# VectorE's edge comparisons and scalings with one operand in PSUM, in a two-layer graph attention kernel

## The chip, the core and the metric

One Trainium2 chip; the program runs on one of its cores. The metric is the device time of one execution in microseconds (us). Times before come from three runs; the profile is of one further execution.

## What is computed

A graph of 6250 nodes and 100000 directed edges, sorted by target node, goes through a block: layer norm and ReLU of x (6250 x 768), two graph attention layers, two dense layers, and x is added at the end. Each attention layer adds an edge from every node to itself. Cut to what matters:

```python
def gat_conv(x, src, dst, W, a_src, a_dst, bias, heads):
    h = (x @ W).reshape(n, heads, -1)
    alpha_s = (h * a_src[None]).sum(-1)
    alpha_d = (h * a_dst[None]).sum(-1)
    e = jax.nn.leaky_relu(alpha_s[src] + alpha_d[dst], 0.2)
    m = jax.ops.segment_max(e, dst, num_segments=n)
    e = jnp.exp(e - m[dst])
    denom = jax.ops.segment_sum(e, dst, num_segments=n)
    alpha = e / (denom[dst] + 1e-16)
    out = jax.ops.segment_sum(h[src] * alpha[:, :, None], dst, num_segments=n)
    return out.reshape(n, -1) + bias
...
h = jnp.maximum(_layernorm(x), 0.0)
h = relu(gat_conv(h, src, dst, W1, a_src1, a_dst1, b1, 4))
h = relu(gat_conv(h, src, dst, W2, a_src2, a_dst2, b2, 1))
return x + relu(h @ Wm1 + bm1) @ Wm2 + bm2
```

## The kernel before

**First stage.** For each of 49 tiles of 128 nodes, x is loaded and normalized (ScalarE writes xn), turned by six TensorE transposes into a PSUM tile `tp` (four, then two; line 202), copied to SBUF by VectorE (`xT`, line 203), and multiplied by W1 together with the score vectors (`h_ps`, line 206). The 256 features of a node, a one for each head and the source scores go as one row of 264 numbers to a table in DRAM.

**Edges.** Each layer then goes over 784 tiles of 128 edges (782 hold edges), eight to a unit. For each tile GpSimd issues one indirect DMA (line 276) that gathers the 128 source rows by the indices in a column of `src_i`, an SBUF tensor, into G (five buffers of one unit each). The code of a turn i gathers unit i, matches unit i-1, weighs unit i-2 and spreads unit i-3; each engine works through its own queue in order, and a scheduler sets that order.

- `match`: VectorE compares a row of the edges' target places, broadcast over the partitions (`drow`, bf16), with the partition number (`pidx_b`, broadcast along the row) into `mask` (128 x 1024 bf16, line 294), and compares `iota` (0 to 127 along the row) with each edge's target place (`dcol`, one column per tile) into `hot` (128 x 1024 f32, line 298). TensorE multiplies `mask` by a window of target factors (`win`) into `e_ps` (PSUM): the target's factor for each edge.
- `weigh`: ScalarE takes two exponentials of the gathered source scores (`e1`, `e2`, lines 316 and 318). VectorE adds up the three bf16 parts of the factor (`rho`), multiplies (`v`), and takes the larger (`w`): the edge's unnormalized weight. In layer 1 `hw` is G times w (128 x 2080 f32, line 332); in layer 2 it is hot times w (128 x 1024 f32, line 328).
- `spread`: TensorE adds the weighted rows into the place of their target (`o_ps`, line 348, two PSUM tiles of four edge tiles each): hot by hw in layer 1, hw by G in layer 2. So G is last read by VectorE's `hw` in layer 1 and by TensorE's products in layer 2, and its buffer is then free for the gather five units later.
- `gather_up`: VectorE carries a running sum, `acc` = `acc` times a column `keep` + `o_ps` (line 363), and ScalarE copies 32 finished rows at a time into `sum` (line 374).

When 128 nodes are complete, further steps follow among the later units. In layer 1: add the node's own edge and divide (`mine`, `all_`, `o`, lines 427 to 434), transpose (`tp`, line 408), ReLU (`rT`), multiply by W2 (`h_ps`, line 441) and store a row of layer 2's table. In layer 2: the same for one head, with the bias added to the residual (`xt`, line 471), two dense layers (`m_ps`, line 484, `mT`, line 488; `y_ps`, line 498), the residual sum (`y`, line 500) and the store. Layer 2 gathers from a table that layer 1's last step completes, so the layers follow each other.

**PSUM** has eight banks of 2 KB per partition. One pool of two buffers per tag served the whole kernel: `tp` (transposes, `e_ps`), `mm` (`h_ps`, `m_ps`), `o` (`o_ps`), `y` (`y_ps`).

Of the kernel before, what the change touches and what calls it, by code (L numbers as in the profile page):

```python
# [9 lines left out]
F32 = mybir.dt.float32  # L10
BF16 = mybir.dt.bfloat16
# [5 lines left out]
P = 128  # L17
# [28 lines left out]
def kernel(  # L46
# [29 lines left out]
    ps = pool("ps", 2, space=bass.MemoryType.PSUM)  # L76

    def bcast(src, n, off=0):
# [72 lines left out]
    def with_scores(wp, W, WT, A, K, H, name):  # L151
# [7 lines left out]
        p = ps.tile([P, K, 2 * H], F32, name="aps", tag="tp")  # L159
# [19 lines left out]
    with tc.tile_pool(name="w1p", bufs=1) as wp, tc.tile_pool(name="x1", bufs=4) as xp, \  # L179
            tc.tile_pool(name="wk1", bufs=3) as wk:  # L180
        w1 = with_scores(wp, W1, W1T, A1, KI, 4, "w1")
        for i in range(NT):
# [21 lines left out]
            h_ps = ps.tile([P, HID + 8], F32, name="h_ps", tag="mm")  # L204
# [52 lines left out]
    def layer_edges(layer, H, steps, prefetch):  # L257

        C = HID // H
        with tc.tile_pool(name=f"pre{layer}", bufs=1) as pre, \  # L260
# [22 lines left out]
            def match(u):  # L283

                if u % 2 == 0:
# [8 lines left out]
                nc.vector.tensor_tensor(mask[:, t0 * P:(t0 + n) * P],  # L294
                                        drow[0][:, u % 2, t0 * P:(t0 + n) * P],
                                        pidx_b.to_broadcast([P, n * P]), ALU.is_equal)
                hot = eg.tile([P, 8, P], F32, name="hot", bufs=3)
                nc.vector.tensor_tensor(  # L298
                    hot[:, t0:t0 + n], iota.unsqueeze(1).to_broadcast([P, n, P]),
                    dcol[:, 8 * u + t0:8 * u + t0 + n].unsqueeze(2).to_broadcast([P, n, P]),  # L300
                    ALU.is_equal)
                e_ps = ps.tile([P, 8, 3 * H], F32, name="e_ps", tag="tp")
                for t in T:
                    g = 2 * u + t // TPG
                    nc.tensor.matmul(e_ps[:, t], mask[:, t * P:(t + 1) * P], win[:, g + 1],  # L305
                                     start=True, stop=True)
                return hot, e_ps

            def weigh(u, G, hot, e_ps):
# [13 lines left out]
                nc.vector.tensor_mul(v[:, T], e2[:, T], rho[:, T])  # L323
# [494 lines left out]
```

## Time and profile before

| | |
|---|---|
| median of the runs | 2580.2 us (2576.93 to 2584.65, 3 runs) |
| the profiled execution | 2569.64 us, span 2567.9 us |
| mean granted TensorE clock | 0.77 |
| TensorE busy (matmul) | 1429.3 us, 56% |
| VectorE busy | 1324.1 us, 52% |
| ScalarE busy | 448.5 us, 17% |
| GpSimd busy | 1761.1 us, 69% |
| DMA | 350.68 MB, mean 137 GB/s |

How to read the rows of the profile: a group's row has line, engine, operation, output and inputs with their sizes and the count, then busy time in us, the mean of one in ns, and after the second bar the idle time of its engine just before these instructions, with what ended it. A timeline's row has start, length (both us), engine, line, operation and, in brackets, the idle time before it and what ended that. PE is TensorE, DVE VectorE, ACT ScalarE, POOL GpSimd, SP the engine that issues most plain DMAs; "issue" is time in which the engine waited for nothing that the profile shows. Matrix products of f32 show two instructions each.

### The profile page before, as it was taken

The page shows a single profiled execution, that of the slowest core. Times are in us where ns is not written, and L with a number is a line of the kernel's source. Part 1 is how long each engine was busy: PE and PEld are TensorE (multiplying, and loading weights), DVE is VectorE, ACT ScalarE, POOL GpSimd, SP SyncE. Part 2 cuts the span into 40 slices and gives each one's busy share as a digit, 9 for nine tenths or more (in the row PEclk, how much of TensorE's full clock was granted, in tenths as well). Part 3 has the DMA queues.
Part 4 walks back from the last instruction along what each step waited for, and adds up shares of the span by engine and source line. Part 5 has one row for each costly group of instructions (what it writes and reads, how often), then busy time and mean ns, then how long its engine had stood idle before and what let it go on. Part 6 is the DMA issues. An engine that isn't in the chain of part 4 may idle for free. (4 is left out here: it accounts for less than half of the span.)

```text
span 2567.9 us, 22404 instructions
## 1 busy us (share of the span) xinstructions
PE 1429.3 (56%) x6784; PEld 1114.5 (43%) x6785; DVE 1324.1 (52%) x2458; ACT 448.5 (17%) x1434; POOL 1761.1 (69%) x1672
## 2 busy tenths in 40 slices
PE   5887335445445445445445464656666666666666
PEld 4665223334334334334334343445444544454444
DVE  5553445554554555555555633455555555555554
ACT  2442111111111111111111111111111111111111
POOL 0000777777777787778787377777777777777770
PEclk9999667677677677677677676877778777877788
DMA  4442444444444444444444445455555555555551
GB/s 164 127 127 74 117 118 127 117 127 129 118 125 130 118 123 131 123 119 127 116 124 121 138 116 154 137 162 168 167 167 167 168 166 167 168 168 166 167 159 57
DMA packets 142758, 350.68 MB, mean 137 GB/s; under 512 B 33570, under 2 KB 60194, under 8 KB 142628
## 3 DMA queue, kind: packets, MB, share of 16 engines
q0 software_dynamic: 75072, 209.10, 31.2%
q1 hardware_dynamic: 65540, 137.21, 16.2%
q10 hardware_dynamic: 2016, 2.85, 0.4%
q8 instruction: 56, 0.92, 0.1%
q14 instruction: 74, 0.61, 0.1%
HBM read 316.53 MB, written 32.50 MB: 136 GB/s over the span
## 5 line engine op out<-in xcount | busy, mean ns | idle before, releaser
L276 POOL DMA_INDIRECT G<-table,src_i x1564 | 1744.3, 1115 | 514.8 <-issue 455.8
L348 PE MATMUL o_ps<-G,hw 128*128 128x258 f32 x1564 | 438.0, 442 | 21.1 <-DVE hw L328 12.8
L363 DVE SCALAR_TENSOR_TENSOR acc<-acc,keep,o_ps 128x260 f32<-128x260 f32 (+1 forms) x390 | 185.6, 476 | 508.3 <-PE o_ps L348 508.0
L348 PE MATMUL o_ps<-hw,hot 128*128 128x260 f32 x1564 | 417.2, 426 | 54.5 <-DVE hw L332 52.3
L348 PEld LDWEIGHTS o_ps<-G,hw 128*128 128x128 f32 x1564 | 354.6, 230 | 109.1 <-issue 23.0
L348 PEld LDWEIGHTS o_ps<-hw,hot 128*128 128x128 f32 x1564 | 337.6, 219 | 123.8 <-DVE hw L332 57.7
L441 PE MATMUL h_ps<-w,rT 128*128 128x258 f32 x196 | 116.4, 699 | 446.8 <-ACT rT L411 446.8
L498 PE MATMUL y_ps<-wm,mT 128*128 128x384 f32 x392 | 180.7, 594 | 314.0 <-DMA G<-table,src_i 276.9
L441 PEld LDWEIGHTS h_ps<-w,rT 128*128 128x128 f32 x196 | 48.8, 307 | 460.2 <-ACT rT L411 459.9
L298 DVE TENSOR_TENSOR hot<-iota,dcol 128x1024 f32<-128x1024 f32 (+1 forms) x196 | 238.0, 1214 | 0.0
L294 DVE TENSOR_TENSOR mask<-drow,pidx_b 128x1024 bf16<-128x1024 bf16 (+1 forms) x196 | 237.3, 1212 | 0.1
L498 PEld LDWEIGHTS y_ps<-wm,mT 128*128 128x128 f32 x392 | 81.5, 222 | 352.8 <-ACT mT L488 319.0
L332 DVE TENSOR_TENSOR hw<-G,w 128x2080 f32<-128x2080 f32 (+1 forms) x98 | 226.8, 2314 | 0.7 <-DMA G<-table,src_i 0.3
L374 ACT ACTIVATE sum<-acc 32x260 f32<-32x260 f32 (+1 forms) x392 | 163.2, 416 | 228.4 <-DVE acc L363 220.9
L318 ACT ACTIVATE e<-G 128x32 f32<-128x32 f32 (+2 forms) x196 | 41.9, 214 | 788.9 <-DMA G<-table,src_i 781.2
L316 ACT ACTIVATE e<-G 128x32 f32<-128x32 f32 (+2 forms) x196 | 42.8, 218 | 778.1 <-DMA G<-table,src_i 682.1
L206 PE MATMUL h_ps<-w,xT 128*128 128x264 f32 x588 | 146.6, 400 | 37.3 <-DVE xT L203 37.3
L206 PEld LDWEIGHTS h_ps<-w,xT 128*128 128x128 f32 x588 | 110.5, 195 | 64.8 <-ACT sd L211 46.1
L408 PE MATMUL tp<-ident,o 128*128 128x128 f32 x196 | 41.9, 298 | 144.3 <-DVE v L323 103.0
L328 DVE TENSOR_TENSOR hw<-hot,w 128x1024 f32<-128x1024 f32 (+1 forms) x98 | 119.2, 1217 | 0.0
L305 PEld LDWEIGHTS <-mask 128*128 128x128 bf16 x1564 | 72.9, 102 | 80.1 <-issue 33.6
L408 PEld LDWEIGHTS tp<-ident,o 128*128 128x128 f32 x196 | 24.4, 147 | 178.8 <-issue 139.4
(384 smaller groups left out, 1002.3 us busy)
## 6 DMA issues: line engine op xcount, KB each, us to landing
drow<-dmod_d SPq DMA_DIRECT2D x98, 512.0 KB, 5.5
xt<-in_x SPq DMA_DIRECT2D x96, 384.0 KB, 3.6
G<-table,src_i POOLq DMA_INDIRECT x1564, 2.8
out<-y SPq DMA_DIRECT2D x48, 384.0 KB, 2.9
table<-row SPq DMA_DIRECT2D x49, 132.0 KB, 1.7
row<-table SPq DMA_DIRECT2D x49, 130.0 KB, 4.6
table<-row SPq DMA_DIRECT2D x49, 129.0 KB, 2.7
row<-table SPq DMA_DIRECT2D x49, 129.0 KB, 2.1
```

The source lines that it names most:

```text
L206: nc.tensor.matmul(h_ps, xT[:, k], w1[:, k], start=(k == 0), stop=(k == KI - 1))
L276: nc.gpsimd.indirect_dma_start(out=G[:, t], out_offset=None, in_=table[layer], in_offset=bass.IndirectOffsetOnAxis(ap=src_i[:, k:k + 1], a ...
L294: nc.vector.tensor_tensor(mask[:, t0 * P:(t0 + n) * P], drow[0][:, u % 2, t0 * P:(t0 + n) * P], pidx_b.to_broadcast([P, n * P]), ALU.is_equal)
L298: nc.vector.tensor_tensor(hot[:, t0:t0 + n], iota.unsqueeze(1).to_broadcast([P, n, P]), dcol[:, 8 * u + t0:8 * u + t0 + n].unsqueeze(2).to ...
L305: nc.tensor.matmul(e_ps[:, t], mask[:, t * P:(t + 1) * P], win[:, g + 1], start=True, stop=True)
L328: nc.vector.tensor_mul(hw[:, T], hot[:, T], w[:, T].to_broadcast([P, n, P]))
L332: nc.vector.tensor_mul(hw[:, T], G[:, T, :RW[1]].rearrange("p t (h c) -> p t h c", h=H), w[:, T].unsqueeze(3).to_broadcast([P, n, H, C + 1]))
L348: nc.tensor.matmul(o_ps, l, r, start=(t == T[0]), stop=(t == T[-1]))
L363: nc.vector.scalar_tensor_tensor(acc, run[0], keep[:, (g + 1) % 4:(g + 1) % 4 + 1], o[half], ALU.mult, ALU.add)
L374: nc.scalar.activation(done[t][r], acc[r], AF.Copy)
L441: nc.tensor.matmul(h_ps, rT[:, k], w2[:, k], start=(k == 0), stop=(k == KH - 1))
L498: nc.tensor.matmul(y_ps, mT[:, j], wm2[:, j, s * half:(s + 1) * half], start=(j == 0), stop=(j == KH - 1))
```

## The change

A copy of `iota` is kept in PSUM (`iota_ps`, f32, one bank). `mask` becomes a tensor-scalar operation on `drow` alone, with `pidx` (f32) as a column of scalars. `hot` is made in layer 1 only, from `iota_ps` and `dcol`. `rho`, `v` and, in layer 1, `w` live in PSUM, in three more parts of `e_ps`, so `hw` of layer 1 multiplies G (SBUF) by w (PSUM). In layer 2 `hot` and `hw` become one operation per edge tile, eight per unit: compare `iota_ps` with a column of `dcol`, times a column of `w`. PSUM is shared out anew: one bank for `iota_ps`, two for `e_ps` (tag `e`), two for `o_ps` and the first stage's `h_ps` (tag `o`), three for all else (tag `n`). The pool is closed before the rarely used general path (`general`), which gets one of its own. The diff, without the general path's:

```diff
-    ps = pool("ps", 2, space=bass.MemoryType.PSUM)
+    edges_stack = ExitStack()
+    ps = edges_stack.enter_context(tc.tile_pool(name="ps", bufs=2, space=bass.MemoryType.PSUM))
...
-    pidx_b = const.tile([P, 1], BF16, name="pidx_b")
-    nc.vector.tensor_copy(pidx_b, pidx)
...
+    iota_ps = ps.tile([P, P], F32, name="iota_ps", bufs=1)
+    nc.vector.tensor_copy(iota_ps, iota)
...
-                p = ps.tile([P, 4, P], F32, name="tp", tag="tp")
+                p = ps.tile([P, 4, P], F32, name="tp", tag="n", bufs=3)
...
-            h_ps = ps.tile([P, HID + 8], F32, name="h_ps", tag="mm")
+            h_ps = ps.tile([P, HID + 8], F32, name="h_ps", tag="o")
...
-                nc.vector.tensor_tensor(mask[:, t0 * P:(t0 + n) * P],
+                nc.vector.tensor_scalar(mask[:, t0 * P:(t0 + n) * P],
                                         drow[0][:, u % 2, t0 * P:(t0 + n) * P],
-                                        pidx_b.to_broadcast([P, n * P]), ALU.is_equal)
-                hot = eg.tile([P, 8, P], F32, name="hot", bufs=3)
-                nc.vector.tensor_tensor(
-                    hot[:, t0:t0 + n], iota.unsqueeze(1).to_broadcast([P, n, P]),
-                    dcol[:, 8 * u + t0:8 * u + t0 + n].unsqueeze(2).to_broadcast([P, n, P]),
-                    ALU.is_equal)
-                e_ps = ps.tile([P, 8, 3 * H], F32, name="e_ps", tag="tp")
+                                        pidx, None, ALU.is_equal)
+                hot = None
+                if layer == 1:
+                    hot = eg.tile([P, 8, P], F32, name="hot", bufs=3)
+                    nc.vector.tensor_tensor(
+                        hot[:, t0:t0 + n], iota_ps.unsqueeze(1).to_broadcast([P, n, P]),
+                        dcol[:, 8 * u + t0:8 * u + t0 + n].unsqueeze(2).to_broadcast([P, n, P]),
+                        ALU.is_equal)
+
+                e_ps = ps.tile([P, 8, 6 * H], F32, name="e_ps", tag="e")
...
-                rho = sm.tile([P, 8, H], F32, name="rho")
-                nc.vector.tensor_reduce(rho[:, T], e_ps[:, T].rearrange("p t (h k) -> p t h k", k=3),
-                                        AX.X, ALU.add)
-                v = sm.tile([P, 8, H], F32, name="v")
+                rho, v, w = (e_ps[:, :, k * H:(k + 1) * H] for k in range(3, 6))
+                nc.vector.tensor_reduce(
+                    rho[:, T], e_ps[:, T, :3 * H].rearrange("p t (h k) -> p t h k", k=3),
+                    AX.X, ALU.add)
                 nc.vector.tensor_mul(v[:, T], e2[:, T], rho[:, T])
-                w = sm.tile([P, 8, H], F32, name="w")
-                nc.vector.tensor_max(w[:, T], v[:, T], e1[:, T])
                 if layer == 2:
+                    w = sm.tile([P, 8, H], F32, name="w")
+                    nc.vector.tensor_max(w[:, T], v[:, T], e1[:, T])
                     hw = eg.tile([P, 8, P], F32, name="hw")
-                    nc.vector.tensor_mul(hw[:, T], hot[:, T],
-                                         w[:, T].to_broadcast([P, n, P]))
+                    for t in tiles(u):
+                        nc.vector.tensor_scalar(hw[:, t], iota_ps, dcol[:, 8 * u + t:8 * u + t + 1],
+                                                w[:, t], ALU.is_equal, ALU.mult)
                 else:
+                    nc.vector.tensor_max(w[:, T], v[:, T], e1[:, T])
                     hw = eg.tile([P, 8, H, C + 1], F32, name="hw")
...
-        p = ps.tile([P, KH, P], F32, name="tp", tag="tp")
+        p = ps.tile([P, KH, P], F32, name="tp", tag="n", bufs=3)
...
-            h_ps = ps.tile([P, HID + 2], F32, name="h_ps", tag="mm")
+            h_ps = ps.tile([P, HID + 2], F32, name="h_ps", tag="n", bufs=3)
...
-            m_ps = ps.tile([P, KH, P], F32, name="m_ps", tag="mm")
+            m_ps = ps.tile([P, KH, P], F32, name="m_ps", tag="n", bufs=3)
...
-                y_ps = ps.tile([P, half], F32, name="y_ps", tag="y")
+                y_ps = ps.tile([P, half], F32, name="y_ps", tag="n", bufs=3)
```

The scheduler orders the instructions anew; the orders that the prediction rests on stand in it.

More of the change, by code (lines that the diff above doesn't have):

```diff
@@ L158, in with_scores @@
         nc.sync.dma_start(a, A.rearrange("(j p) h -> p j h", p=P))
-        p = ps.tile([P, K, 2 * H], F32, name="aps", tag="tp")
+        p = ps.tile([P, K, 2 * H], F32, name="aps", tag="e")
         for k in range(K):
@@ L534, in general @@
     KH = HID // P
-    const, ps, dram, bcast, ident, sd, table = (
-        v[k] for k in ("const", "ps", "dram", "bcast", "ident", "sd", "table"))
+    const, dram, bcast, ident, sd, table = (
+        v[k] for k in ("const", "dram", "bcast", "ident", "sd", "table"))
     NTP = NT + 1
@@ L545, in general @@
         wk = pool("gwk", 1)
+        ps = pool("gps", 2, space=bass.MemoryType.PSUM)
         gdram = pool("gdram", 1, space=bass.MemoryType.DRAM)
@@ L769, in general @@
             for s in range(2):
-                y_ps = ps.tile([P, half], F32, name="y_ps", tag="y")
+                y_ps = ps.tile([P, half], F32, name="y_ps", tag="e")
                 for j in range(KH):
```

13 lines of the change are left out of this document (7 added, 6 removed).

## The prediction

> **What bounds the kernel now.** I read the page first: busy time in slices and the costliest groups. Then the view of one line, for the gather.
>
> ```profile
> POOL 0000777777777787778787377777777777777770
> ...
> L276 POOL DMA_INDIRECT G<-table,src_i x1564 | 1744.3, 1115 | 514.8 <-issue 455.8
> ```
>
> ```profile
> L276 POOL DMA_INDIRECT G<-table,src_i  x1564: 942/946/3459, 254.0 to 2508.2; - x196
> ...
>   issue: 455.8, 1496
>   DVE parts L230: 35.4, 1
> ```
>
> GpSimd issues 1564 gathers, one per tile of 128 edges, and has no other work from 254.0 us on. The idle time before them is 0.30 us each (455.8 over 1496), plus one gap of 35.4 us between the layers. So GpSimd never waits for buffers: from 254 to 2509.7 us the span is gathers laid end to end, and the slices of 7 and 8 are only that pause. The median gather takes 0.946 us but the mean 1.115: some are stretched. The windows by stage, for this line alone (length, busy time, count, clock, DMA share, GB/s), place that:
>
> ```profile
> 0.00:254.00 254.00, 0.00 (x0) 0.99 0.39 122
> 254.00:1418.60 1164.60, 926.65 (x782) 0.71 0.45 123
> 1418.60:1454.10 35.50, 0.07 (x1) 0.79 0.24 75
> 1454.10:2509.70 1055.60, 817.56 (x782) 0.78 0.56 162
> 2509.70:2567.90 58.20, 0.00 (x0) 0.83 0.14 49
> ```
>
> 782 gathers at 0.946 us would be 739.8 us. Layer 1 carries 926.65 - 739.8 = 186.9 us of stretch and layer 2 77.8: 264.7 us in all. The timeline of layer 1 tells whose it is:
>
> ```profile
> 1002.54 0.95 POOL L276 DMA_INDIRECT G<-table,src_i  x1 [0.31 <-issue]
> ...
> 1003.09 2.31 DVE L332 TENSOR_TENSOR hw<-G,w 128x2080 f32<-128x2080 f32 x1
> 1003.80 2.42 POOL L276 DMA_INDIRECT G<-table,src_i  x1 [0.30 <-issue]
> 1005.32 1.21 DVE L298 TENSOR_TENSOR hot<-iota,dcol 128x1024 f32<-128x1024 f32 x1
> ...
> 1006.52 0.95 POOL L276 DMA_INDIRECT G<-table,src_i  x1 [0.31 <-issue]
> ...
> 1007.08 1.21 DVE L294 TENSOR_TENSOR mask<-drow,pidx_b 128x1024 bf16<-128x1024 bf16 x1
> 1007.77 1.34 POOL L276 DMA_INDIRECT G<-table,src_i  x1 [0.30 <-issue]
> ```
>
> A gather that starts while VectorE runs `hw` ends at 1006.22, 0.82 us after `hw` does (1005.40); the one that starts in `mask` ends at 1009.11, again 0.82 after 1008.29. The gather that is under way when `hw` starts keeps its 0.95. So the gather needs something at its start that these instructions hold to their end, and the stretch is the end of the VectorE instruction less the gather's start less 0.13 us. Not every VectorE instruction does it. In layer 2:
>
> ```profile
> 2003.81 0.48 DVE L363 SCALAR_TENSOR_TENSOR acc<-acc,keep,o_ps 128x258 f32<-128x258 f32 x1
> 2003.88 0.95 POOL L276 DMA_INDIRECT G<-table,src_i  x1 [0.30 <-issue]
> ...
> 2019.77 1.09 DVE L500 TENSOR_TENSOR y<-y_ps,xt 128x384 f32<-128x384 f32 x2
> ...
> 2020.69 0.95 POOL L276 DMA_INDIRECT G<-table,src_i  x1 [0.30 <-issue]
> ```
>
> `acc` reads one tensor from SBUF, one from PSUM and a column of scalars from SBUF; `y` reads one of each memory. Gathers that start inside them are not stretched. `hw`, `hot` and `mask` read two tensors from SBUF.
>
> The Trainium skill, "SBUF — State Buffer", section "Who interferes with whom", has both halves of this: a VectorE instruction with two SBUF inputs contends with a GpSimd instruction that reads SBUF, and one with at most one does not. The same section infers that `tensor_tensor` does not stall a DMA issued from GpSimd; by that sentence the change would win nothing on the gathers, and the 2.42 us row decides against it.
>
> **The change, part by part.** Gathers, first term. After the change `hot` reads PSUM and SBUF, `hw` of layer 1 reads G from SBUF and its weights from PSUM, `hw` of layer 2 reads one PSUM tensor and two scalar columns, and `mask` reads one SBUF tensor. If only two SBUF tensors block, all of them leave the list: -264.7 us, for GpSimd is the path and nothing covers it.
>
> What stays, second term. Instructions with two SBUF tensors are still there, and their phases move. Rows for the sizes:
>
> ```profile
> L298 DVE TENSOR_TENSOR hot<-iota,dcol 128x1024 f32<-128x1024 f32 (+1 forms) x196 | 238.0, 1214 | 0.0
> L294 DVE TENSOR_TENSOR mask<-drow,pidx_b 128x1024 bf16<-128x1024 bf16 (+1 forms) x196 | 237.3, 1212 | 0.1
> L332 DVE TENSOR_TENSOR hw<-G,w 128x2080 f32<-128x2080 f32 (+1 forms) x98 | 226.8, 2314 | 0.7 <-DMA G<-table,src_i 0.3 <-DVE acc L363 0.3 <-DVE v L323 0.2
> ...
> L471 DVE TENSOR_TENSOR xt<-xt,bm2b 128x768 f32<-128x768 f32 x49 | 46.5, 948 | 5.4 <-DMA xt<-in_x 5.4
> ...
> L427 DVE TENSOR_TENSOR mine<-row,own 128x260 f32<-128x260 f32 x49 | 20.6, 419 | 0.0
> ...
> L194 DVE TENSOR_SCALAR shift<-mv,rstd 128x1 f32<-128x1 f32 x49 | 10.3, 211 | 1.5
> ...
> L123 DVE TENSOR_SCALAR far<-f 98x1024 f32<-98x1024 f32 x1 | 0.7, 686 | 0.0
> ```
>
> An instruction of L us at a random phase of the gathers' rhythm (0.946 + 0.30 = 1.25 us) costs (L - 0.13)²/2.5 on average; the most is L - 0.13. `xt` (0.948): 0.27 x 49 = 13 us, at most 40. `mine` (0.419) and its two neighbours of the same size: 0.033 x 147 = 5, at most 43. The one in layer 2 like `mine`: 2, at most 18. `mask` is now a one-tensor bf16 operation, which the trace lacks. From `hot` and `hw`: (2314 - 1214)/1056 = 1.04 ns an element and 0.15 us fixed. `far`, one f32 tensor, runs two elements in that time (0.686); a bf16 mask should be no slower, and if it halves once more it takes 0.41. So 0.41 to 0.69; I take 0.41. If it still blocks at a gather's start, 0.03 x 196 = 6, at most 55. Together 26, from 0 to 156. These phases are locked to the gathers, so each is all or nothing; I take 25.
>
> `hot` from PSUM and `hw` of layer 1: 258 elements in `acc` cost 0.48 us from PSUM against 0.419 for 260 in `mine`, so +0.06 each at most. Layer 2's `hot` (98 x 1.21) and `hw` (98 x 1.22) become 8 x 98 pieces of 128 elements: 0.13 us of elements at least, `shift`'s 0.211 plus 0.13 = 0.34 at most, so 1.1 to 2.7 us in place of 2.4 per unit. All of it lies beside the gathers; VectorE has room:
>
> ```profile
> 300.00:1400.00 1100.00, 507.94 (x2415) 393.47 (x2416) 567.80 (x944) 150.11 (x543) 875.18 (x739) 0.71 0.46 123
> ```
>
> (busy PE, weight loads, VectorE, ScalarE, GpSimd: VectorE 567.8 of 1100.) A unit (8 gathers) of layer 1 takes 1164.6/97.75 = 11.9 us and holds 6.2 us of VectorE work; the mask's 0.8 goes and 0.12 comes: 5.5, against 10 us of gathers. If that cover were gone, it would add up to 0.12 us a unit, 12 us per layer.
>
> The new PSUM pools, third term. Transposes get three buffers. TensorE in the first stage, two node tiles before the change (tp: transposes of the normalized x; h_ps: x times W1):
>
> ```order
> L202 MATMUL tp_519<-ident_63,xn_516 128x128 x4
> L202 MATMUL tp_525<-ident_63,xn_516 128x128 x2
> L206 MATMUL h_ps_529<-w1_132,xT_518 128x264 x6
> L202 MATMUL tp_558<-ident_63,xn_555 128x128 x4
> L202 MATMUL tp_564<-ident_63,xn_555 128x128 x2
> L206 MATMUL h_ps_568<-w1_132,xT_557 128x264 x6
> ```
>
> and the same two tiles after it:
>
> ```order
> L204 MATMUL tp_519<-ident_63,xn_516 128x128 x4
> L204 MATMUL tp_525<-ident_63,xn_516 128x128 x2
> L204 MATMUL tp_558<-ident_63,xn_555 128x128 x4
> L208 MATMUL h_ps_529<-w1_132,xT_518 128x264 x6
> L204 MATMUL tp_564<-ident_63,xn_555 128x128 x2
> L208 MATMUL h_ps_568<-w1_132,xT_557 128x264 x6
> ```
>
> Four transposes of the second tile move ahead of the first tile's product, into the wait for VectorE's copy xT:
>
> ```profile
> 103.34 0.82 PE L202 MATMUL tp<-ident,xn 128*128 128x128 f32 x6
> ...
> 104.82 2.91 PE L206 MATMUL h_ps<-w,xT 128*128 128x264 f32 x12 [0.66 <-DVE xT L203]
> ...
> 107.56 0.82 PE L202 MATMUL tp<-ident,xn 128*128 128x128 f32 x6
> ```
>
> and its group:
>
> ```profile
> L206 PE MATMUL h_ps<-w,xT 128*128 128x264 f32 x588 | 146.6, 400 | 37.3 <-DVE xT L203 37.3
> ```
>
> A tile takes 107.56 - 103.34 = 4.22 us. In a pair, 0.55 us of transposes now fills the first 0.66 and the second 0.66 goes: 1.2 us a pair, 24 pairs, 29 us; the waits bound it at 37.3. VectorE, ScalarE and the x loads must keep up with 3.6 us a tile, so between 0 and 30; I take -22. It counts in full: gathers wait for the last tile's row.
>
> Layer 2 on VectorE, one unit before (v, w: weights; acc: running sums; xt: the residual):
>
> ```order
> L320 TENSOR_REDUCE rho_11915<-e_ps_11829 128x8
> L471 TENSOR_TENSOR xt_11855<-xt_11855,bm2b_8370 128x768
> L323 TENSOR_TENSOR v_11917<-e2_11913,rho_11915 128x8
> L363 SCALAR_TENSOR_TENSOR acc_11923<-acc_11858,keep_80,o_ps_11886 128x258
> L325 TENSOR_TENSOR w_11919<-v_11917,e1_11911 128x8
> L294 TENSOR_TENSOR mask_11963<-drow_11896,pidx_b_72 128x1024
> L328 TENSOR_TENSOR hw_11921<-hot_11827,w_11919 128x1024
> L363 SCALAR_TENSOR_TENSOR acc_11926<-acc_11923,keep_80,o_ps_11891 128x258
> ```
>
> and after:
>
> ```order
> L325 TENSOR_REDUCE e_ps_11247<-e_ps_11247 128x8
> L370 SCALAR_TENSOR_TENSOR acc_11349<-acc_11281,keep_80,o_ps_11309 128x258
> L328 TENSOR_TENSOR e_ps_11247<-e2_11334,e_ps_11247 128x8
> L370 SCALAR_TENSOR_TENSOR acc_11352<-acc_11349,keep_80,o_ps_11314 128x258
> L331 TENSOR_TENSOR w_11338<-e_ps_11247,e1_11332 128x8
> L478 TENSOR_TENSOR xt_11278<-xt_11278,bm2b_8076 128x768
> L334 TENSOR_SCALAR hw_11340<-iota_ps_74,dcol_89,w_11338 128x128 x8
> ```
>
> Both sums now stand ahead of the weights, so `hw` waits for all 8 of the previous unit's o_ps products, not 4. That matters because G has five buffers, and layer 2's products release them:
>
> ```profile
> 2028.99 0.94 POOL L276 DMA_INDIRECT G<-table,src_i  x1 [0.30 <-issue]
> ...
> 2032.14 0.22 ACT L316 ACTIVATE e<-G 128x8 f32<-128x8 f32 x1 [8.94 <-DMA G<-table,src_i]
> ...
> 2032.77 1.65 PE L498 MATMUL y_ps<-wm,mT 128*128 128x384 f32 x2 [7.44 <-DMA G<-table,src_i]
> 2033.00 0.41 ACT L374 ACTIVATE sum<-acc 32x258 f32<-32x258 f32 x1
> ...
> 2034.21 4.81 PE L348 MATMUL o_ps<-G,hw 128*128 128x258 f32 x16
> ...
> 2040.24 0.95 POOL L276 DMA_INDIRECT G<-table,src_i  x1 [0.30 <-issue]
> ```
>
> A unit's last gather ends at 2029.93 and its rows land at 2032.14; TensorE, held in its queue till then, does y_ps and then the o_ps products that end at 2039.02. They free the buffer that the gather of 2040.24 fills: 1.2 us to spare, of 10.3. Unstretched gathers come at 8 x 1.25 + 0.3 = 10.3 us too. On ScalarE, what follows such a landing was, before (mT: the two halves of the hidden layer that y_ps reads; e1, e2: exponentials of the gathered scores):
>
> ```order
> L316 ACTIVATE e1_12114<-G_11944 128x8
> L318 ACTIVATE e2_12116<-G_11944 128x8
> L488 ACTIVATE mT_11934<-m_ps_11929,bm1c_8368 128x128 x2
> L374 ACTIVATE sum_11852<-acc_11926 32x258
> L477 ACTIVATE o_11942<-all__11938,rden_11940 128x256
> ```
>
> and is now:
>
> ```order
> L323 ACTIVATE e2_12410<-G_12234 128x8
> L495 ACTIVATE mT_12224<-m_ps_12219,bm1c_8074 128x128
> L381 ACTIVATE sum_12139<-acc_12216 32x258
> L495 ACTIVATE mT_12224<-m_ps_12219,bm1c_8074 128x128
> L321 ACTIVATE e1_12408<-G_12234 128x8
> ```
>
> A sum (0.41 us) moved between the two mT, so y_ps and the products come up to 0.4 us later, and of the 1.2 us some 0.8 is left, every second unit. Fourth term: 0 to 1 us x 49; I take +5.
>
> **Sum.** -264.7 + 25 - 22 + 5 = -256.7 on the profiled execution's 2569.6 us: 2313. The median of the runs shown is 10.6 higher (2580.2): 2323. Gap and tail (35.5 and 58.2 us) hold a few VectorE steps each and stay within 1 or 2.
>
> **The rivals.**
>
> Full lock by the mask (0.12). A fast one-tensor operation SBUF to SBUF could hold more than the read at the gather's start, so that any overlap counts: three quarters of the masks meet a gather, and 196 x 0.41 = 80 is the most, 40 to 75 more than forecast: about 2380. No row shows such an operation over all partitions beside a gather. The Trainium skill, same section, says this of `tensor_scalar` in its two-port modes: whichever starts first blocks the other for the whole instruction. By its rule this rival is right; no run here shows it yet.
>
> The buffers bind (0.10). If the chain in layer 2 costs 1 to 2 us more a pair than the 1.2 to spare, gathers wait: 49 to 98 us, about 2370 to 2420. For: the small margin. Against: the masks give back 0.8 us of VectorE.
>
> The change doesn't do what it says (0.05): any long VectorE read of SBUF blocks. Then only the shorter masks and layer 2's `hw` help: by (L - 0.13)² masks are a sixth of layer 1's stretch (31 us) and at most all of layer 2's goes; with the first stage some 105 less, about 2475. Against: `acc` and `y` above.
>
> Slower (0.03): PSUM read again and again, as `hot` and layer 1's `hw` do (3104 elements a unit), may be slow; no row shows such a read. Of the 5.5 us the rest is about 2. VectorE becomes the bound above 10 us a unit, 2.6 ns an element, and cancels the gains in layer 2 and stage one (about 75 us) above 11.9 + 75/98 = 12.7, or 3.4 ns, over three times the 1.04 of `hot`. At 3.5 ns the time is 2600. `acc` and `y` read PSUM at normal speed.
>
> Nothing moves: 0.02. A difference under 0.3% counts as none, about what a measurement of this kernel can tell.
>
> **The numbers.** Forecast 0.68, between 2285 (no stretch left, 30 us in stage one) and 2385 (60 us left, 10 in stage one, 20 for the buffers). With the full lock and the lower half of the buffers' case, 2280 to 2405 holds 8 in 10. Faster 0.95, same 0.02, slower 0.03.
>
> **What would show it.** Right: mean gather under 0.98 us, the first near 232 us, `hot` and layer 1's `hw` at 1.2 to 1.3 and 2.3 to 2.4, still 0.30 before each gather. Wrong: gathers ending 0.82 after a mask or `hot`; idle time before gathers put down to o_ps (buffers); first gather still at 254; `hot` above 2.5 us.

## The result, and the profile after

The changed kernel takes 2301.35 us (median of 4 runs, 2299.53 to 2303.36), beside 2581.75 us for the kernel before on the same chip: a ratio of 0.8916, 95% interval 0.8899 to 0.8932. The profiled execution spans 2301.6 us, against 2567.9 before. The forecast was 2323 us.

The page of the changed kernel, the slices of GpSimd and the group of the gather (busy time, mean ns | idle time before them):

```profile
POOL 0001777777777777777772777777777777777770
...
L278 POOL DMA_INDIRECT G<-table,src_i x1564 | 1490.3, 953 | 535.0 <-issue 478.5
```

The two slices of 8 are gone, and the mean gather takes 0.953 us (1.115 before), a hair over the median of 0.946. The view of that line:

```profile
L278 POOL DMA_INDIRECT G<-table,src_i x1564: 940/946/1625, 222.0 to 2242.8; - x196
...
  issue: 478.5, 1506
  ACT win L241: 36.0, 1
  PE o_ps L355: 11.3, 37
```

The longest gather takes 1.625 us (3.459 before), the first starts at 222.0 us, and 37 idle times are now put down to o_ps. The windows by stage, for this line alone (length, busy time, count, clock, DMA share, GB/s):

```profile
0.00:222.00 222.00, 0.00 (x0) 0.98 0.44 140
222.00:1207.70 985.70, 747.75 (x782) 0.77 0.53 145
1207.70:1243.70 36.00, 0.05 (x1) 0.78 0.24 74
1243.70:2243.70 1000.00, 742.41 (x782) 0.81 0.57 171
2243.70:2301.60 57.90, 0.07 (x1) 0.83 0.14 50
```

782 gathers at 0.946 us are 739.8, and their 781 pauses of 0.303 are 236.6. Layer 1 so has 8.0 us of stretch and 1.3 of further idle time; layer 2 has 2.6 of stretch and 1000.0 - 742.4 - 236.6 = 21.0 us of further idle time, where the kernel before had 1.4. Term by term, in us against the profiled execution of before:

| term | predicted | measured |
|---|---|---|
| stretch that goes, less what stays | -264.7 + 25 | -254.1 (10.6 stay) |
| first stage | -22 | -32.0 |
| idle time before gathers of layer 2 | +5 | +19.6 |
| gap and tail | 0 | +0.2 |
| sum | -256.7 | -266.3 |

A stretch of layer 1 where `hw`, `hot` and the mask all meet gathers:

```profile
699.36 2.32 DVE L339 TENSOR_TENSOR hw<-G,e_ps 128x2080 f32<-128x2080 f32 x1
700.08 0.95 POOL L278 DMA_INDIRECT G<-table,src_i  x1 [0.30 <-issue]
701.33 0.94 POOL L278 DMA_INDIRECT G<-table,src_i  x1 [0.30 <-issue]
701.59 1.22 DVE L302 TENSOR_TENSOR hot<-iota_ps,dcol 128x1024 f32<-128x1024 f32 x1
702.58 0.94 POOL L278 DMA_INDIRECT G<-table,src_i  x1 [0.30 <-issue]
```

Two gathers start inside `hw` and one inside `hot`, and each keeps its 0.95 us; before, the gather that started 0.7 us into `hw` took 2.42. In all, 165 gathers of layer 1 start in an `hw` and 85 in a `hot`, and none of them is stretched. The durations of these instructions, from the groups:

```profile
L334 DVE TENSOR_SCALAR hw<-iota_ps,dcol,w 128x128 f32<-128x128 f32 x782 | 257.5, 402 | 0.0
...
L339 DVE TENSOR_TENSOR hw<-G,e_ps 128x2080 f32<-128x2080 f32 (+1 forms) x98 | 226.3, 2309 | 0.4 <-DMA G<-table,src_i 0.2
...
L302 DVE TENSOR_TENSOR hot<-iota_ps,dcol 128x1024 f32<-128x1024 f32 (+1 forms) x98 | 119.0, 1215 | 0.0
...
L296 DVE TENSOR_SCALAR mask<-drow,pidx 128x1024 bf16<-128x1024 bf16 (+1 forms) x196 | 94.5, 483 | 0.8 <-DMA drow<-dmod_d 0.7
```

`hot` and layer 1's `hw` take what they took from SBUF (1.214 and 2.314 us): VectorE was not made faster there; what changed is that gathers no longer wait for it. The mask fell from 1.21 to 0.48 us. A piece of layer 2's `hw` costs 257.5/782 = 0.33 us.

The first stage, TensorE alone:

```profile
99.18 2.84 PE L208 MATMUL h_ps<-w,xT 128*128 128x264 f32 x12
101.85 1.26 PE L204 MATMUL tp<-ident,xn 128*128 128x128 f32 x10
103.33 2.91 PE L208 MATMUL h_ps<-w,xT 128*128 128x264 f32 x12 [0.22 <-DVE xT L205]
106.07 0.38 PE L204 MATMUL tp<-ident,xn 128*128 128x128 f32 x2
106.29 2.84 PE L208 MATMUL h_ps<-w,xT 128*128 128x264 f32 x12
```

Two tiles take 106.29 - 99.18 = 7.11 us (8.44 before), and one wait of 0.22 us is left in a pair.

Where layer 2 now waits, on GpSimd, ScalarE and TensorE (in brackets the idle time before a row):

```profile
1867.38 0.22 ACT L323 ACTIVATE e<-G 128x8 f32<-128x8 f32 x1 [7.28 <-DMA G<-table,src_i]
1867.50 0.35 ACT L495 ACTIVATE mT<-m_ps,bm1c 128x128 f32<-128x128 f32 x1
1867.88 0.41 ACT L381 ACTIVATE sum<-acc 32x258 f32<-32x258 f32 x1
...
1867.91 2.93 PE L505 MATMUL y_ps<-wm,mT 128*128 128x384 f32 x4 [6.74 <-ACT mT L495]
...
1868.32 0.37 ACT L495 ACTIVATE mT<-m_ps,bm1c 128x128 f32<-128x128 f32 x1
...
1870.62 4.56 PE L355 MATMUL o_ps<-G,hw 128*128 128x258 f32 x16
...
1875.93 0.94 POOL L278 DMA_INDIRECT G<-table,src_i  x1 [0.79 <-issue]
```

The gather of 1875.93 paused 0.79 us in place of 0.30. It starts 0.75 us after the o_ps products end (1870.62 + 4.56 = 1875.18). Over layer 2, 40 gathers pause longer, one in every second unit, and 38 of them start 0.75 us after the last o_ps product: it is the ring of five buffers.

### The profile page after: what moved, and what is told of

Read it like the earlier page. It is cut to its first block, busy times and chain, and to the rows that moved or that the text cites. A ratio compares the mean times of both kernels' runs of the same rounds, so it can differ in the third digit from the quotient of the medians.

```text
span 2301.6 us, 23617 instructions
## 1 busy us (share of the span) xinstructions
PE 1429.1 (62%) x6784; PEld 1113.7 (48%) x6785; DVE 1210.0 (53%) x3044; ACT 464.7 (20%) x1434; POOL 1507.1 (65%) x1672
## 3 DMA queue, kind: packets, MB, share of 16 engines
q1 hardware_dynamic: 65540, 137.21, 17.7%
## 5 line engine op out<-in xcount | busy, mean ns | idle before, releaser
L278 POOL DMA_INDIRECT G<-table,src_i x1564 | 1490.3, 953 | 535.0 <-issue 478.5
L355 PE MATMUL o_ps<-G,hw 128*128 128x258 f32 x1564 | 415.4, 425 | 5.8 <-DVE hw L334 5.6
L505 PE MATMUL y_ps<-wm,mT 128*128 128x384 f32 x392 | 211.7, 678 | 303.5 <-ACT mT L495 285.2
L448 PE MATMUL h_ps<-w,rT 128*128 128x258 f32 x196 | 100.7, 667 | 285.8 <-ACT rT L418 285.7
L323 ACT ACTIVATE e<-G 128x32 f32<-128x32 f32 (+2 forms) x196 | 43.2, 221 | 1067.4 <-DMA G<-table,src_i 932.0
L334 DVE TENSOR_SCALAR hw<-iota_ps,dcol,w 128x128 f32<-128x128 f32 x782 | 257.5, 402 | 0.0
L339 DVE TENSOR_TENSOR hw<-G,e_ps 128x2080 f32<-128x2080 f32 (+1 forms) x98 | 226.3, 2309 | 0.4 <-DMA G<-table,src_i 0.2
L208 PE MATMUL h_ps<-w,xT 128*128 128x264 f32 x588 | 144.3, 397 | 12.6 <-DVE xT L205 12.6
L208 PEld LDWEIGHTS h_ps<-w,xT 128*128 128x128 f32 x588 | 110.4, 195 | 34.8 <-issue 16.7
L302 DVE TENSOR_TENSOR hot<-iota_ps,dcol 128x1024 f32<-128x1024 f32 (+1 forms) x98 | 119.0, 1215 | 0.0
L296 DVE TENSOR_SCALAR mask<-drow,pidx 128x1024 bf16<-128x1024 bf16 (+1 forms) x196 | 94.5, 483 | 0.8 <-DMA drow<-dmod_d 0.7
L310 PE MATMUL e_ps<-win,mask 128*128 128x12 bf16 (+1 forms) x1564 | 68.0, 167 | 32.0 <-DVE w L331 18.0
```

Of the source, the lines that this page charges most:

```text
L208: nc.tensor.matmul(h_ps, xT[:, k], w1[:, k], start=(k == 0), stop=(k == KI - 1))
L278: nc.gpsimd.indirect_dma_start(out=G[:, t], out_offset=None, in_=table[layer], in_offset=bass.IndirectOffsetOnAxis(ap=src_i[:, k:k + 1], a ...
L296: nc.vector.tensor_scalar(mask[:, t0 * P:(t0 + n) * P], drow[0][:, u % 2, t0 * P:(t0 + n) * P], pidx, None, ALU.is_equal)
L302: nc.vector.tensor_tensor(hot[:, t0:t0 + n], iota_ps.unsqueeze(1).to_broadcast([P, n, P]), dcol[:, 8 * u + t0:8 * u + t0 + n].unsqueeze(2) ...
L310: nc.tensor.matmul(e_ps[:, t, :3 * H], mask[:, t * P:(t + 1) * P], win[:, g + 1], start=True, stop=True)
L334: nc.vector.tensor_scalar(hw[:, t], iota_ps, dcol[:, 8 * u + t:8 * u + t + 1], w[:, t], ALU.is_equal, ALU.mult)
```

## The experiments

The theory: a VectorE instruction that reads two tensors from SBUF holds the start of a gather until it ends. The first rival: the gain comes from less VectorE work (shorter masks) and from other phases (where in the gathers' rhythm an instruction starts), not from where operands lie. For each run the table gives its median, when the first gather starts, the stretch per layer, and layer 2's idle time before gathers beyond 0.30 us each. The kernel before, measured beside e1 to e12, took 2575.8 to 2578.9 us, and 2581.8 beside the changed one; so medians that lie within some 6 us of each other are told apart by the other columns, from one trace each, more than by the time. A gather counts as starting in an instruction when over 0.13 us of that is left: with less, it ends as it would anyway.

| kernel | us | first gather | stretch 1 | stretch 2 | idle 2 |
|---|---|---|---|---|---|
| before | 2581.8 | 254.0 | 186.9 | 77.9 | 1.4 |
| changed | 2301.4 | 222.0 | 8.0 | 2.7 | 20.9 |
| e1: `hot` from SBUF | 2338.2 | 221.2 | 43.5 | 2.7 | 20.6 |
| e2: w in SBUF | 2436.5 | 221.7 | 142.7 | 2.2 | 21.9 |
| e3: mask of two tensors | 2373.8 | 222.8 | 39.2 | 65.1 | 1.3 |
| e4: before, new pools only | 2564.1 | 223.0 | 201.6 | 87.7 | 1.6 |
| e5: layer 2's iota in SBUF | 2299.6 | 222.5 | 8.1 | 16.7 | 1.3 |
| e6: six buffers | 2296.8 | 222.5 | 6.7 | 20.3 | 1.3 |
| e7: a long one-tensor form more | 2464.1 | 223.0 | 20.9 | 42.7 | 125.8 |
| e8: six buffers, no `xt` | 2291.6 | 222.6 | 5.9 | 9.5 | 1.2 |
| e9: layer 2 in two steps | 2291.6 | 221.7 | 6.0 | 11.8 | 1.3 |
| e10: layer 2 from SBUF | 2378.7 | 222.1 | 9.9 | 96.4 | 1.3 |
| e11: e9 and no `xt` | 2283.5 | 222.1 | 6.8 | 2.9 | 1.3 |
| e12: e9 and half of `xt` | 2289.3 | 221.1 | 8.9 | 5.2 | 1.4 |

**e1, `hot` from SBUF.** One operand is put back:

```diff
-                        hot[:, t0:t0 + n], iota_ps.unsqueeze(1).to_broadcast([P, n, P]),
+                        hot[:, t0:t0 + n], iota.unsqueeze(1).to_broadcast([P, n, P]),
```

> The changed kernel (2301 us) with one operand put back: layer 1's hot reads its iota from SBUF again, so it reads two SBUF tensors. Theory (operands decide: two SBUF tensors hold the gather's start to the instruction's end): hot keeps its 1.22 us, and gathers that start in it end 0.82 us after it. At a random phase of the 1.25 us rhythm (1.22 - 0.13) squared / 2.5 = 0.47 us each, 98 times: +46 us, 2347; it can lock to 0 or to 1.09 x 98 = 107. Rival (the gain came from less VectorE work and other phases, not from where operands lie): hot takes the same time, so 2301 within 5 us.

Measured: 2338.2 us, 36.9 more. All 77 gathers that start in a `hot` end 0.82 us after it, and stretch by 33.8 us in all; `hot` takes 1.22 us as before. The first rival falls.

**e2, w in SBUF.** Layer 1's weights go back to a tile in SBUF:

```diff
                 else:
+                    w = sm.tile([P, 8, H], F32, name="w")
                     nc.vector.tensor_max(w[:, T], v[:, T], e1[:, T])
```

> The changed kernel with layer 1's weights w in SBUF again, so that hw (2.31 us) reads two SBUF tensors; all else as changed. Theory (operands): 2.31 us is longer than the rhythm of 1.25, so every hw meets a start, and the stretch is 2.18 us less a phase between 0 and 1.25: 1.56 on average x 98 = 153 us, from 91 to 214; 2454 us (2392 to 2515). The kernel before showed 133. Rival (less work, other phases): 2301 within 5 us.

Measured: 2436.5 us, 135.1 more; of 98 gathers that start in an `hw`, 95 end 0.82 us after it. From its timeline:

```profile
708.65 2.33 DVE L340 TENSOR_TENSOR hw<-G,w 128x2080 f32<-128x2080 f32 x1
709.00 2.81 POOL L278 DMA_INDIRECT G<-table,src_i  x1 [0.30 <-issue]
...
711.29 1.22 DVE L302 TENSOR_TENSOR hot<-iota_ps,dcol 128x1024 f32<-128x1024 f32 x1
712.11 0.94 POOL L278 DMA_INDIRECT G<-table,src_i  x1 [0.30 <-issue]
```

The gather inside `hw` ends at 711.81, 0.83 after it (710.98); the one inside `hot`, whose iota is in PSUM, is not touched. Both cases stand in one kernel, side by side.

**e3, mask of two tensors.** The mask is as before the change (and `pidx_b` is made again):

```diff
-                nc.vector.tensor_scalar(mask[:, t0 * P:(t0 + n) * P],
+                nc.vector.tensor_tensor(mask[:, t0 * P:(t0 + n) * P],
                                         drow[0][:, u % 2, t0 * P:(t0 + n) * P],
-                                        pidx, None, ALU.is_equal)
+                                        pidx_b.to_broadcast([P, n * P]), ALU.is_equal)
```

> The changed kernel with the mask as before the change: a tensor_tensor of two SBUF tensors, 1.21 us in place of 0.48. Theory (operands): 0.47 us x 196 = 92 us at random phases, less the 4 us that the short masks cost now; the kernel before showed 70. So 2370 to 2390, where locked phases 2300 to 2510. Rival (VectorE's work decides): 0.73 us more work a unit lies beside 10 us of gathers, of which VectorE is busy 5.4: 2301 within 5 us.

Measured: 2373.8 us, 72.4 more; all 177 gathers that start in a mask end 0.82 us after it. Stretch grew by 94 us, and 19.6 came back: gathers that are stretched come later than the buffers, and layer 2's wait is gone.

**e4, the pools alone.** The kernel before with the change's tags and buffers of PSUM, all operands where they were; against the kernel before, in the first stage (and likewise for the other tiles of PSUM):

```diff
-                p = ps.tile([P, 4, P], F32, name="tp", tag="tp")
+                p = ps.tile([P, 4, P], F32, name="tp", tag="n", bufs=3)
...
-            h_ps = ps.tile([P, HID + 8], F32, name="h_ps", tag="mm")
+            h_ps = ps.tile([P, HID + 8], F32, name="h_ps", tag="o")
```

> The kernel before with only the new PSUM pools (three buffers for the transposes, no operand moved). Theory: the first gather starts at 222 in place of 254 us, gathers are stretched as before (265 us within 15), and nothing else moves: 2581.8 - 32 = 2550 us. Rival (the pools also bring the buffer wait of layer 2): 20 us less gain, 2570, if the wait shows although stretched gathers come later than the buffers do.

Measured: 2564.1 us, 14.3 under the kernel before as measured beside it, a ratio of 0.9932 (0.9903 to 0.9962). The first gather starts 31 us earlier as expected, but the stretch rose from 264.7 to 289.3 us: the phases moved. The rival's wait hardly shows (1.6 us), so neither forecast holds. As long as gathers are stretched, what another stage wins is not what the end wins.

**e5, layer 2's iota in SBUF.**

```diff
-                        nc.vector.tensor_scalar(hw[:, t], iota_ps, dcol[:, 8 * u + t:8 * u + t + 1],
+                        nc.vector.tensor_scalar(hw[:, t], iota, dcol[:, 8 * u + t:8 * u + t + 1],
```

> The changed kernel with the 8 pieces of layer 2's hw reading iota from SBUF: one SBUF tensor and two scalar columns, f32. Theory A (a VectorE instruction that reads a single SBUF tensor holds gathers too when it runs in a fast form, as the new mask does): pieces get shorter than 0.33 us and gathers that start in one end 0.82 us after that piece; at most 0.2 us each for the 170 to 250 that start in a piece: +5 to +30 us, 2306 to 2331. Theory B (only two SBUF tensors hold): no gather ends 0.82 us after a piece beyond chance, 2301 within 4 us.

Measured: 2299.6 us. Theory A holds as a mechanism: eight pieces take 2.14 us in place of 2.63, and 43 of the 56 gathers that start in one end 0.82 us after it (1 of 137 with PSUM, where none is stretched). But such a piece is short, and they stretch by 2 us only. The order of the work moved too: no waits for buffers (19.6 us less), `xt` now in the way of 45 gathers (13.6 us). PSUM won no time for this operand; that the two other effects nearly cancel was not foreseen.

**e6, six buffers.**

```diff
-                tc.tile_pool(name=f"g{layer}", bufs=5) as gp, \
+                tc.tile_pool(name=f"g{layer}", bufs=5 if layer == 1 else 6) as gp, \
```

> The changed kernel with six buffers for the gathered rows of layer 2 in place of five. Theory (the 0.48 us before every second unit's sixth gather is the wait for the buffer that o_ps gives back): all 39 of these waits go, 20.9 us of idle time becomes 1.3: 2301 - 20 = 2281 us. Rival (the wait is of another kind, such as the gathers in flight or SyncE's queue): the pauses stay at 0.79, 2301 within 3 us.

Measured: 2296.8 us, 4.5 less where 20 were expected. The waits are gone as predicted, and so the rival is wrong. But now the rhythm is steady, and `xt` falls on the same gather in nearly every second unit:

```profile
1775.82 0.95 DVE L478 TENSOR_TENSOR xt<-xt,bm2b 128x768 f32<-128x768 f32 x1
1776.17 1.41 POOL L278 DMA_INDIRECT G<-table,src_i  x1 [0.30 <-issue]
```

43 gathers that start in `xt` are stretched by 19.4 us (the expectation of e8 counts 38 and 17.7). The expectation had left out that a wait sets the phase.

**e7, a long one-tensor form.** Which rule is it, two tensors or the shared way to SBUF? An instruction of the mask's form is added to each unit, over twice the elements, into a buffer that nobody reads:

```diff
+                spare = eg.tile([P, 2, 8 * P], BF16, name="spare")
+                nc.vector.tensor_scalar(spare[:, :min(2, NU - u + u % 2)],
+                                        drow[0][:, :min(2, NU - u + u % 2)],
+                                        pidx, None, ALU.is_equal)
```

> The changed kernel with one more VectorE instruction per unit, in the mask's form but over 2048 elements, into a buffer that nobody reads (196 of them; nothing that the output needs changes). By the masks of 768 and 1024 elements (0.397 and 0.484 us) it takes 0.83 us. Theory A (one SBUF tensor in the fast form holds a gather's start to its end, as 24 of the 27 gathers that started in a mask show): (0.83 - 0.13) squared / 2.5 = 0.20 us x 196 = 38 us, 2340, locked phases 2301 to 2438. Theory B (only two SBUF tensors hold; the masks' 0.82 is chance): 2301 within 5. Rival C (a full lock: also gathers under way are held): every instruction that meets a gather costs up to 0.83, 80 to 160 us, and gathers under way when it starts last longer than 0.95.

Measured: 2464.1 us, 163 more and above the range expected, but only 53 of it is stretch. From its timeline:

```profile
1090.54 1.08 POOL L278 DMA_INDIRECT G<-table,src_i  x1 [0.30 <-issue]
1090.76 0.75 DVE L300 TENSOR_SCALAR spare<-drow,pidx 128x2048 bf16<-128x2048 bf16 x1
...
1511.86 0.73 DVE L300 TENSOR_SCALAR spare<-drow,pidx 128x2048 bf16<-128x2048 bf16 x1
...
1512.29 1.12 POOL L278 DMA_INDIRECT G<-table,src_i  x1 [0.30 <-issue]
...
1517.13 0.48 DVE L296 TENSOR_SCALAR mask<-drow,pidx 128x1024 bf16<-128x1024 bf16 x1
...
1517.46 0.96 POOL L278 DMA_INDIRECT G<-table,src_i  x1 [0.30 <-issue]
1517.52 0.75 DVE L300 TENSOR_SCALAR spare<-drow,pidx 128x2048 bf16<-128x2048 bf16 x1
```

The gather of 1512.29 starts inside the long instruction and ends at 1513.41, 0.82 after it: so did 68 of 71. Theory B falls, a single SBUF tensor in this form holds a gather's start. The gather of 1090.54 had started 0.22 us before the long instruction and ends at 1091.62, 0.11 after it (1091.51): a gather under way is held too, near its end. The gather of 1517.46 shows that only these two places count. It starts in a mask and ends 0.81 us after that mask; the long instruction covers most of the rest, but ends at 1518.27, 0.81 us into the gather, and adds nothing. So rival C has its sign (gathers under way that last longer than 0.95), but not its price: 111 gathers end 0.12 us after a mask or long instruction that began behind their start, for 17.4 us, where C had 80 to 160. The starts in the long instruction cost 10.5 us, those in masks 5.6, and 26.0 come from 44 gathers that start in `xt`, whose phase moved. Most of the other 110 us, 105, is idle time before gathers of layer 2: 0.75 us more on VectorE (the long instruction's mean) moved the order of work there, and the ring of five buffers answered with waits of about 3 us in every second unit. Which of the two, the time or the order, did most of that was not separated.

**e9 and e10, layer 2 in two steps.** The merging is undone: `hot` is built for layer 2 too, and `hw` is `hot` times w. In e9 each has one operand in PSUM, in e10 both read SBUF alone, as before the change. The weighing:

```diff
...
-                    for t in tiles(u):
-                        nc.vector.tensor_scalar(hw[:, t], iota_ps, dcol[:, 8 * u + t:8 * u + t + 1],
-                                                w[:, t], ALU.is_equal, ALU.mult)
+                    nc.vector.tensor_mul(hw[:, T], hot[:, T],
+                                         w[:, T].to_broadcast([P, n, P]))
```

> The changed kernel with layer 2's matches and weighing as two instructions again, each with one operand in PSUM (hot from iota_ps, hw as hot times w with w in PSUM): the merging undone, the memories kept. Theory (only the memories matter; VectorE's 2.44 in place of 2.63 us a unit lies beside the gathers): 2301 us within 5, and layer 2 has no gather that ends 0.82 us after a hot or hw. Rival (hw takes 1.2 in place of 2.6 us on the way to the o_ps products that free the buffers): the 20 us of waits go, 2281 us, or less of it if xt locks to the gathers' starts again.

> The changed kernel with layer 2's hot and hw as before the change: two instructions, each with two SBUF tensors; layer 1 and the mask as changed. Theory (operands decide): two instructions of 1.22 us a unit meet starts: at random phases 0.47 x 196 = 92 us, where the kernel before showed 38.5 in this layer (hot 26.7, hw 11.8); stretched gathers then hide the buffers' 20 us. 2301 - 20 + 38 to 92 = 2319 to 2373; 2320 taken. Rival (merged or not, the work beside the gathers doesn't matter): 2301 within 5 us.

Measured: e9 2291.6 us and e10 2378.7, 6 above the range expected. No gather in e9 is stretched by `hot` or `hw` of layer 2 (82 start in a `hot`, 77 in an `hw`); in e10 they cost 60.5 (`hw`) and 15.8 us (`hot`), and the masks, whose phase moved, 12.8 (3.1 in e9). The memories decide again. And the merging, apart from them, did not pay: e9's waits for buffers are gone, 19.6 us, of which `xt` and others take back 9, and it is 9.7 us faster than the changed kernel. The rival of e9 was right in direction. The order of layer 2's work changed along with it (the y_ps products now stand together, where four of them stood right ahead of o_ps), so whether the shorter `hw` or the order ended the waits was not separated.

**e8, e11 and e12, what is left in layer 2.** `xt` (0.95 us, two SBUF tensors) is the last long one. In e8 (six buffers) and e11 (two steps, five buffers) TensorE adds the bias and `xt` goes:

```diff
...
-            nc.vector.tensor_add(xt, xt, bm2b)
...
+                nc.tensor.matmul(y_ps, ones_r, bm2r[:, s * half:(s + 1) * half],
+                                 start=True, stop=False)
...
```

In e12 (two steps) half of the bias lies in the rest of iota's bank of PSUM:

```diff
...
-            nc.vector.tensor_add(xt, xt, bm2b)
+            half = OUT_DIM // 2
+            nc.vector.tensor_add(xt[:, :half], xt[:, :half], bm2_ps)
+            nc.vector.tensor_add(xt[:, half:], xt[:, half:], bm2b[:, half:])
```

> Six buffers in layer 2, and no xt instruction: the bias bm2 is added by TensorE, as a product of a column of ones with the bias row, ahead of each y_ps. With six buffers alone the pauses went (idle time beyond 0.30 us a gather 20.9 to 1.3 us), but 38 gathers then started in xt and were stretched by 17.7 us: 2296.8. Theory (the two were one after the other, and xt is the only long instruction with two SBUF tensors left in layer 2): without xt nothing is stretched and nothing waits: 2296.8 - 17.7 = 2279 us, layer 2 at 782 x 1.249 = 979 us. Rival (TensorE's extra products, 98 of 384 columns, bring the wait back): 2290 to 2300, with idle time before gathers put down to o_ps.

> Layer 2 in two steps (as in the run of 2291.6 us that undid the merging) and no xt instruction (bias by TensorE, as in the run with six buffers); five buffers. Theory (in the two-step kernel nothing waits for buffers and xt causes 9.0 of the 17.8 us of stretch; the bias products cost 3.3 us after the last gather, 61.1 in place of 57.8): 2291.6 - 9.0 + 3.3 = 2286 us. Rival A (what xt leaves, other instructions' phases take up: a sum of stretch near 18 us again): 2292 to 2295. Rival B (the extra products bring the buffers' waits back): 2300 or more.

> Layer 2 in two steps, and xt in two instructions of 384 columns, the first with the bias in PSUM (in the rest of iota's bank), the second with both tensors in SBUF. Theory (operands): the first holds nothing; the second, some 0.55 us, stretches at most 0.42 us and at a random phase 0.07 us, so 9.0 us of xt's stretch become some 3; no work after the last gather is added: 2291.6 - 6 = 2286 us, between 2283 and 2303. Rival (phases take up what is freed): 2291 within 2.

Measured: 2291.6, 2283.5 and 2289.3 us. In e8 other instructions took `xt`'s place (28 gathers that start in masks 4.1 us, 17 in `all_` 4.0, and 25 that masks hold at their end 2.0), and the end after the last gather is 3.6 us longer than in the changed kernel. The time lies in the rival's range, but not for its reason: nothing waits for buffers (1.2 us). In e11 neither happened (59.3 us after the last gather, 59.6 in e9): its layer 2 takes 980.6 us, the 976.4 of unstretched gathers and their pauses nearly exactly. In e12 layer 2's stretch fell by 6.6 us as expected, and layer 1's grew by 2.9 with nothing changed there; the time fits its rival too. e11's windows by stage, for the gather's line:

```profile
222.00:1206.50 984.50, 746.43 (x782) 0.76 0.53 145
...
1241.80:2222.40 980.60, 742.54 (x782) 0.78 0.59 174
```

e11 beats both kernels: 0.8864 of the kernel before (0.8843 to 0.8885), and 17.9 us under the changed one.

## Why the prediction was right, and where it was off

**The mechanism is shown.** "If only two SBUF tensors block, all of them leave the list": `hot` and both `hw` did. Putting an operand back in SBUF brings the stretch back, at the same duration (e1, e2, and e10 against e9). The rival that any long VectorE read of SBUF blocks is out by the 250 gathers of layer 1 that start in `hw` or `hot` without harm. The rival that a PSUM operand read again and again is slow is out by 1.215 and 2.309 us; so is the 0.06 us that the prediction allowed for it.

**The list was not quite the rule.** The mask reads one SBUF tensor, and still 24 of the 26 gathers that start in it end 0.82 us after it. The prediction had this as a bound ("If it still blocks at a gather's start, 6"); it costs 4 us, because the mask is short. So two of the signs that the prediction named for being wrong came, at a small size: gathers that end 0.82 us after a mask, and idle time put down to o_ps. e7 shows the price of a longer instruction, and that this form holds a gather at a second place, near its end. The rival of the full lock thus had part of the mechanism: it counted any overlap, 40 to 75 us more, where two places of a gather count, and in the changed kernel the second one costs 0.6 us (5 gathers). The Trainium skill, "SBUF — State Buffer", section "Who interferes with whom", names this form (`tensor_scalar` in its two-port modes) as the exception to what it says of one SBUF input, and says that the first to issue blocks the other for the whole instruction. (The prediction's first sentence on that section leaves the exception out; its rival brings it in.) The traces agree where VectorE comes first, as the gather waits for the instruction's end at both places; where the gather comes first, the mask waits for a part of it only (last section).

**The residual term was 14 us too high.** `xt` was put at 13 us from a random phase. In the changed kernel only 5 gathers start in it, for 2.4 us; in e6 it is 43, for 19.4, and in e5 45, for 13.6. The phase is locked, so it is set by what comes before and not by chance; the prediction said so, and its mean was then only a guess.

**The buffers' term was mis-sized.** +5 was taken, +19.6 came, still within its bounds of 0 to 49. Two steps failed. "1.2 us to spare" counted from the end of the products to the gather's start; but a gather that is held starts 0.75 us after that end, so that only 0.45 were to spare. And "up to 0.4 us later", from the sum between the two mT, missed that two more of y_ps's products now go ahead of o_ps: x4 in 2.93 us, where the row of before shows x2 in 1.65. From the landing to the last o_ps product it is 7.80 us (1867.38 to 1875.18) against 6.88 (2032.14 to 2039.02): 0.92 more, less the 0.45, is 0.47 us; 40 of them are 19 us.

**The first stage was 10 us too low.** The pair was put at 7.2 us and came at 7.11. The -22 was a discount for VectorE and ScalarE, which kept up. Even the end of 30 was passed: the waits of h_ps shrink by 24.7 us (37.3 to 12.6), the first transpose starts 1.5 us earlier, and TensorE is busy for 6 us less with the same products and transposes (173.5 in place of 179.5); why that is was not traced.

**The step from the profiled execution to the median was wrong.** 10.6 us were added because the kernel before's median lay that far above its profiled execution. That was a place within the kernel before's own spread (2569.6 to 2584.7), and a spread doesn't carry over: the runs of the changed kernel lie within 4 us, and the profiled execution (2303.4) is the slowest of them. Of the 22 us by which 2323 was too high the terms made 9.6, this step 10.6, and the place of the profiled execution 2.0. That the terms made no more is luck: two of them were too cautious, by 14.4 and 10 us, and the buffers' took 14.6 back. Why the kernel before spreads so was not tried.

**The merging was not judged.** The prediction costed its pieces (0.13 to 0.34 us; 0.33 came) and found them covered. e9, without them, waits for no buffer and is 9.7 us faster (with another order of work, too), and e5 shows that their operand need not be in PSUM.

**The parts don't add up.** Putting back `hot` costs 37 us, w 135, the mask 72, layer 2's pair 77, and the pools alone bring 14: 335 in all, where the change brings 280. Each is measured among phases of its own, and stretched gathers hide layer 2's 20 us of waits.

## What to carry to other kernels

Where GpSimd issues gathers back to back, look at which VectorE instructions its long ones start in, and give these an operand in PSUM: `hot` and layer 1's `hw` lost no VectorE time by it (the one-tensor pieces of layer 2 did, 2.63 us against 2.14 for eight). One SBUF tensor is not always enough: the mask's form still holds gathers, so keep such an instruction short. The price of an instruction L us long is at most L - 0.13 per gather that starts in it, unless another of the kind follows at once: the longest gather before took 3.46 us, through an `hw` and the `hot` behind it. The phase sets how many gathers start in it, so what is freed at one place can be taken at the next. Estimates from random phases came near for the instructions that stand in every unit (92 us for e3's masks, which cost 90.0; 153 for e2's `hw`, 140.8), but not for `xt` in every second one: 13 us by the estimate, from 2.4 in the changed kernel to 26.0 in e7. When a rhythm gets faster, count the spare time of each ring of buffers from the moment a held transfer would start, not from the end of the work that frees it.

## What the runs showed of the hardware beside that

The hold near a gather's end belongs to the one-tensor form. In the eleven kernels with the new mask, 138 gathers started unheld, met a mask or e7's long instruction that began 0.14 to 0.46 us behind their start, and were still under it at 0.83 us: all 138 end 0.12 us after it. Another 87, whose instruction ended before 0.83 us, keep their 0.946. Of 408 gathers of all fourteen kernels that met an instruction with two SBUF tensors in the first of these ways, 402 keep theirs: that kind holds the start alone.

The lock works the other way too. In e2:

```profile
374.02 0.95 POOL L278 DMA_INDIRECT G<-table,src_i  x1 [0.30 <-issue]
...
374.56 0.65 DVE L296 TENSOR_SCALAR mask<-drow,pidx 128x1024 bf16<-128x1024 bf16 x1
```

A mask that starts 0.54 us into a gather takes 0.65 us in place of 0.48, and ends 1.19 us after the gather's start. In the eleven kernels, all 201 masks that start between 0.46 and 0.67 us after an unstretched gather's start end 1.19 us after it, that is 0.71 + 0.48: they wait for the gather's 0.71. (65 others that start at 0.46 to 0.50 us, 42 of them in e7, keep their 0.48, and the gather ends 0.12 us after them.) Masks that start in its first 0.4 us or after 0.72 keep 0.48. The `tensor_tensor` mask of before shows no such delay (52 that start 0.5 to 0.6 us in take 1.207 to 1.220 us).
